# Half 1's second spectral stage as a class of its own, in buffers that the output stage shares

## The chip, the cores and the metric

The kernel runs on one core of a Trainium2 chip. The metric is the device time of one launch in microseconds (us). Before the change it was 2658.32 us, the median of three runs (2653.32 to 2668.18). The engines are called PE (matrix products), PEld (its weight loads), ACT (scalar engine), DVE (vector engine), POOL (GpSimd) and SP (the engine that issues most DMAs).

## The reference, cut to what matters

Layer 0 (a gated attention over 256 rows) makes x1, an image of 256 tokens of 256 x 128 pixels. Layer 1 takes those tokens through an attention in spectral space and two Fourier layers, and adds the result to x1. The change lies in the second Fourier layer (`mix_*[1]`) and the final sum:

```python
def spectral_conv(x, wr, wi, bias, out_hw):
    xf = jnp.fft.rfft2(x, norm='forward')
    top = jnp.einsum('bixy,ioxy->boxy', xf[:, :, :h, :m2], w[:, :, :h])
    bot = jnp.einsum('bixy,ioxy->boxy', xf[:, :, H - h:, :m2], w[:, :, h:])
    ...                                  # 32 x 16 modes, 4 channels in, 4 out
    return jnp.fft.irfft2(of, s=(Ho, Wo), norm='forward') + bias[:, None, None]

h1 = fno_layer(h0, mix_wr[0], ..., norm=True, act=True)
h2 = fno_layer(h1, mix_wr[1], ..., norm=True)
out = instance_norm(h2, mon_w, mon_b) + attn        # attn: normed sum of attention and tokens
```

A Fourier layer is a spectral product, normed, plus a 1x1 mixing of the four channels of a group ("skip"). Only 512 modes of each token are kept. The transforms are matrix products with small tables of sines and cosines; the norm of the spectral part is worked out from its modes.

## The kernel before, in words

The 256 tokens lie in two halves of 128, half 0 and half 1, one token to a partition. An image of a half is cut into 16 blocks of 2048 pixels (NB), each of two halves of 1024 (HB). In layer 1 a half goes through these steps, each a Python generator whose instructions are written out by hand in the order in which the engines are to take them (`manual_schedule`, L1890, for PE, ACT, DVE, POOL and SP): an engine takes its instructions, and SP its DMA issues, in the order of the program.

- `first_images` (L1582) makes the first layer's image block by block, transforms each block along the width into spectra and writes them to DRAM: psA (L1672) is copied by ACT to yA (L1674), and POOL issues the write to Yd (L1675), 16 image rows a block, 256 KB.
- `second_modes` (L1681) reads those spectra back (`load`, L1688, SP) into tiles YT of chunk c (four chunks of four frequencies) and half of the rows hc; `forward` (L1700) transforms along the height (L1706, into PSUM, copied by DVE to F, L1712); `mix_modes` (L1438) multiplies by the weights; `mixed` (L1475) copies the two accumulators to Z and squares them; `norm` (L1489) sums the energies; `synth_modes` (L615) transforms each chunk back along the height and writes it to Gd2 in DRAM (L664, SP and ACT issue two DMAs each); between the chunks stand the covariance (L1749), the blocks for the skip product (L1767), and at the end the per-token scale and shift (L1776 to L1786).
- `output` (L1788) makes the second layer's image of a block from the first layer's (skip, L1274) and the modes in Gd2 (image, L1259), scales it (L1795, ACT), adds w (L1801, DVE), and POOL issues the output DMA (L1802).

`mix_modes` works in products: DVE (every third one POOL) multiplies F by a weight, broadcast, into a tile (L1457), and PE adds it into an accumulator in PSUM by a product with the identity (L1470). For half 1 it takes two chunks at a time, two products to a tile; a group below is such a tile with its two accumulating products on PE.

w is lam * y + x1, where y is the attention's image (yd in DRAM) and x1 is read again. For half 1 class `Output1` makes it. `load(k)` (L1833) issues y and then x1 of 1024 pixels on SP (L1839, L1843); `add(k)` (L1846) makes w on DVE in one instruction (L1848). For k = 0 to 3 `ahead` (L1851) does this earlier, beside `second_modes`: ACT scales y (L1859) and POOL adds (L1863). In `run` (L1865) SP first issues the modes of four blocks (`modes`, four DMAs each, L1283), then `load` of k = 4 to 7, and then after each block b the modes of block b + 4, the adds of all loaded k up to 2b + 5, and the loads of 2b + 8 and 2b + 9.

A tile comes from a pool under a tag with a number of buffers. A new tile of a tag takes a buffer when the last reader of the tile that had it is done; the instruction that first writes it waits for that, also where that reader stands later in the program, on another engine. When a pool closes, its memory goes to pools opened later, and their first writers wait for its last users. Half 1's stage before uses pools of its own, opened after `with yctx` (L1899) has closed the pool xp, in which half 0's output and the loads lay: mp3 (YT and the transformed chunks, tag gt, two buffers), op1 (y under yo with two buffers, x1 under xo with five, two gs) and, for the output, op2 (three more yo, three more xo, two more gs).

The lines that set the order around the change:

```python
m1 = second_modes(1, wp, tiles(wp), Banks(psq, "q"), [(wp, "gt", 2)], [(wp, "gt", 2)] * 4)
next(m1)
o1.more = op
ahead = o1.ahead()
next(ahead)
next(ahead)
next(m1)
...
run(iter(lambda: next(m1), 1.2))
run(ahead)
run(m1)
```

Of the kernel before, what the change touches and what calls it, by code (L numbers as in the profile page):

```python
# [30 lines left out]
def rsqrt(nc, pool, out, var, eps, tag):  # L31

    shape = list(out.shape)
    ve = pool.tile(shape, FP, tag=tag + "_ve", name=tag + "_ve")
    nc.vector.tensor_scalar(ve, var, eps, None, ALU.add)
    r = pool.tile(shape, FP, tag=tag + "_r", name=tag + "_r")
    nc.scalar.activation(r, ve, AF.Sqrt)
    nc.vector.reciprocal(r, r)
    n = pool.tile(shape, FP, tag=tag + "_n", name=tag + "_n")
    nc.vector.tensor_mul(n, r, r)  # L40
    nc.vector.tensor_mul(n, n, ve)
    nc.vector.tensor_scalar(n, n, -0.5, 1.5, ALU.mult, ALU.add)
    nc.vector.tensor_mul(out, r, n)
# [544 lines left out]
def layer1(tc, I, C, ident, x1d, upool, U, Q2, groups, out):  # L588
# [9 lines left out]
    with ExitStack() as ctx:  # L598
# [983 lines left out]
        def first_images(a, wp, yp, psk, pst, first=None):  # L1582
# [44 lines left out]
            for b in range(17):  # L1627
# [37 lines left out]
                if b > 0:  # L1665
# [9 lines left out]
                    nc.gpsimd.dma_start(  # L1675
# [4 lines left out]

        def second_modes(a, wp, mk, psum, gts, yts):  # L1681

            h = halves[a]
            ym, yv, ra, lam, r2, rho, sig, _, kap, c0, hm, hv = (h.col[:, k : k + 1] for k in range(12))
# [29 lines left out]
            if a:  # L1714
                for hc in range(2):
                    for c in range(2):
                        load(c, (hc,))

                nc.scalar.activation(h.col[:, 12:13], yv, AF.Sqrt)
            else:  # L1720
                load(0)
# [3 lines left out]
            load(2 if a else 1)  # L1725
            yield 4.0
            forward(1)
            if not a:
                load(2)
# [14 lines left out]
            for c in range(4):  # L1744
                if c == 2:
                    ps = psum.tile(f"cvps_{a}")
                    for i in range(4):
                        for r in range(2):
# [7 lines left out]
                            queues=(nc.sync if a else nc.gpsimd, nc.scalar))  # L1756
# [4 lines left out]
                if c == 1:  # L1761
                    run(tail)

                    for i in range(4):
                        r = slice(32 * i, 32 * i + 32)
                        v = h.row[r, 0:P].rearrange("k (b d x) -> k b d x", b=2, d=2)
                        nc.vector.tensor_tensor(  # L1767
                            h.bl0[r].rearrange("k (b d x) -> k b d x", b=2, d=2),
                            v[:, :: (-1 if i & 2 else 1), :: (-1 if i & 1 else 1)],
                            bc(bc(blk[1][r, r], 1, 2), 1, 2), ALU.mult,  # L1770
                        )
            rs, krs, left = (h.col[:, k : k + 1] for k in (12, 14, 15))
# [3 lines left out]
            nc.vector.tensor_mul(krs, ps[:, 0:1], rs)  # L1776
            nc.vector.scalar_tensor_tensor(hv, krs, 4.0, hv, ALU.mult, ALU.add)
            nc.vector.tensor_add(hv, hv, left)
            rsqrt(nc, wp, kap, hv, EPS, "rq")
            nc.vector.tensor_mul(kap, kap, ch[:, 4:5])  # L1780
            nc.vector.tensor_mul(krs, kap, rs)
            nc.vector.tensor_mul(c0, hm, kap)
            nc.vector.tensor_sub(c0, ch[:, 5:6], c0)
            nc.vector.tensor_add(c0, c0, an[:, 1:2])
            nc.vector.tensor_mul(r2, ym, lam)
            nc.vector.tensor_sub(c0, c0, r2)  # L1786
# [40 lines left out]
        class Output1:  # L1827


            def __init__(self, wp):  # L1830
                self.wp, self.ld, self.w = wp, {}, {}

            def load(self, k):  # L1833
                px = slice(k * HB, (k + 1) * HB)
                old = k < 5 or k % 5 < 2
                y = (self.wp if old else self.more).tile(
                    [P, HB], FP, tag="yo", name=f"y4_{k}", bufs=2 if old else 3
                )
                nc.sync.dma_start(y, ydv[:, 1, px])  # L1839
                x = (self.wp if k % 8 < 5 else self.more).tile(  # L1840
                    [P, HB], FP, tag="xo", name=f"x4_{k}", bufs=5 if k % 8 < 5 else 3
                )
# [8 lines left out]
            def ahead(self):  # L1851

                for half in range(2):
                    for k in (2 * half, 2 * half + 1):
                        self.load(k)
                    yield
                    for k in (2 * half, 2 * half + 1):
                        y = self.ld[k][1]
                        nc.scalar.activation(y, y, AF.Identity, scale=halves[1].col[:, 3:4])  # L1859
                    yield  # L1860
                    for k in (2 * half, 2 * half + 1):
                        self.w[k], y = self.ld.pop(k)
                        nc.gpsimd.tensor_tensor(self.w[k], self.w[k], y, ALU.add)  # L1863

            def run(self, psk, more):  # L1865
                self.more = more
                gs = {}

                def modes(b):
                    gs[b] = (self.wp if b % 4 < 2 else self.more).tile(  # L1870
                        [P, 4, P], FP, tag="gs", name=f"gs3_1_{b}", bufs=2
                    )
                    load_modes(gs[b], halves[1].Gd2, b)

                for b in range(4):
                    modes(b)
                for k in range(4, 8):
                    self.load(k)
# [11 lines left out]
        with tc.manual_schedule(engines=COMPUTE | {ENG.SP}):  # L1890
# [8 lines left out]
            with yctx:  # L1899
                U1 = 24  # L1900
                with tc.tile_pool(name="mp0", bufs=1) as wp:
                    y1 = y_blocks(1, br, 0, U1, Sums(wp))
                    weave((2.4 * t for t in first_modes(0, wp, tiles(wp), bq, [(wp, "gt", 1)])), y1)
                    halves[0].sums = True
                    run(y1)
                with tc.tile_pool(name="hp0", bufs=2) as wp:
                    run(first_images(0, wp, xp, bq, br))
                with tc.tile_pool(name="mp1", bufs=1) as wp:
                    y1 = y_blocks(1, br, U1, 32)
                    next(y1)  # L1910
                    m0 = second_modes(
                        0, wp, tiles(wp), bq, [(xp, "xt", 3)], [(wp, "gt", 1)] * 3 + [(xp, "xt", 3)]
                    )
                    weave((2.4 * next(m0) for _ in range(3)), y1)
                    run(y1)
                    m1 = first_modes(
                        1, wp, Tiles(F=(xp, "yt", 2), f=(xp, "yt", 2), m=(xp, "gs", 3)), br, [(xp, "xt", 3)]
                    )
                    next(m1)
                    for k, _ in enumerate(iter(lambda: next(m0), None)):  # L1920
                        if k % 4 == 3:
                            next(m1)
                    for _ in m0:
                        next(m1, None)
                    o0 = output_0(bq)
                    next(o0)
                    y2 = wp.tile([P, NB], FP, tag="gt", name="y2_0", bufs=1)
                    nc.sync.dma_start(y2, ydv[:, 1, 0:NB])
                    run(m1)
                    g2 = wp.tile([P, 4, P], FP, tag="m", name="gs2_1_0", bufs=2)  # L1930
                    next(o0)
                    load_modes(g2, halves[1].Gd1, 0)
                    next(o0)
                with tc.tile_pool(name="hp1", bufs=2) as hp:
                    next(o0)
                    next(o0)
                    due, begun = 0.0, False
                    for done in first_images(1, hp, xp, bq, br, ([y2[:, 0:HB], y2[:, HB:]], g2)):
                        if not done:
                            due += 0.9  # L1940
                            begun = due > 0
                        if begun:
                            next(o0, None)
                        if done and begun:
                            due -= 1.0
                    run(o0)
            pz.release_now()
            with tc.tile_pool(name="op1", bufs=2, side="right") as op:
                o1 = Output1(op)
                with tc.tile_pool(name="mp3", bufs=1) as wp, tc.tile_pool(  # L1950
                    name="mpq3", bufs=8, space=PSUM
                ) as psq:
                    m1 = second_modes(1, wp, tiles(wp), Banks(psq, "q"), [(wp, "gt", 2)], [(wp, "gt", 2)] * 4)
                    next(m1)
                    o1.more = op
                    ahead = o1.ahead()
                    next(ahead)
                    next(ahead)
                    next(m1)
                    next(m1)  # L1960
                    next(ahead)
                    next(ahead)
                    run(iter(lambda: next(m1), 1.2))
                    run(ahead)
                    run(m1)
                with tc.tile_pool(name="opk1", bufs=8, space=PSUM) as psk, tc.tile_pool(
                    name="op2", bufs=1
# [166 lines left out]
```

## Time and profile before

| what | us |
|---|---|
| median of three runs (lowest, highest) | 2658.32 (2653.32, 2668.18) |
| the profiled execution | 2673.89 |
| its span, from the first to the last instruction | 2672.1 |
| last yA copy (L1674) ends | 2464.1 |
| first mixing product (L1457) begins | 2478.3 |
| last accumulating product (L1470) ends | 2504.0 |
| last instruction of the shift (L1786) ends | 2525.2 |
| first gs load for the output issued (L1283) | 2527.3 |
| first image product of the output (L1259) | 2529.6 |
| last output DMA issued (L1802) | 2665.6 |

The page's first line has the span; its part 1 gives the busy time of each engine, and part 2 cuts the span in 40 slices of 66.8 us. Layer 0 fills the first half, to about 1360 us; there PE, DVE and POOL are busy nearly all the time. Layer 1's spectral stages follow. The change touches what runs from about 2440 us to the end. In a timeline a line gives the start, the length, the engine, the line, what it writes and reads, the count of merged instructions, and in brackets the idle time before it with what ended it. PE's records are two for each product here. SPq, ACTq and POOLq are the engines' DMA issues; the time of a DMA itself is its landing, which the chain of work shows as "DMA out<-in".

### The profile page before, as it was taken

To read this page: it belongs to the slowest core of one execution; us is meant where nothing else is said; L and a number is where in the kernel's file an instruction comes from. 1 tells how busy PE (TensorE), PEld (TensorE's weight loads), DVE (VectorE), ACT (ScalarE), POOL (GpSimd) and SP (SyncE) were. 2 spreads that over 40 slices of the span, in tenths; PEclk is the share of its full clock that TensorE was granted. 3 is DMA by queue.
4 is the path that set the end of the run, shared out by engine and by line. 5 is a ranking of instruction groups with operands and counts; after the bars stand their busy time and mean duration, and the time that the engine had idled before them with its cause. 6 is when DMAs were issued, how large, how long until landed. Compare 5 with 4: busy or idle time off the path is not lost. (4 is left out here: it accounts for less than half of the span.)

```text
span 2672.1 us, 88760 instructions
## 1 busy us (share of the span) xinstructions
PE 2426.5 (91%) x37572; PEld 1549.0 (58%) x37572; DVE 2027.5 (76%) x2886; ACT 1421.3 (53%) x2718; POOL 1488.8 (56%) x1042
## 2 busy tenths in 40 slices
PE   6699999999999999999997999998979978898754
PEld 6555655555656555565554567786755456444533
DVE  6799999999999999999996457566546654465455
ACT  0278888888888888888884122001016401555232
POOL 1199999999999999999994012002136411111211
PEclk8899999999999999999998989999989988899855
DMA  9755666556566666565652011888877764997598
GB/s 348 222 91 100 107 105 107 101 104 105 105 105 109 107 107 108 102 106 103 109 101 63 4 58 47 274 272 289 297 264 265 239 223 149 332 359 260 192 386 344
DMA packets 1017925, 459.02 MB, mean 172 GB/s; under 512 B 831094, under 2 KB 947273, under 8 KB 1011128
## 3 DMA queue, kind: packets, MB, share of 16 engines
q1 hardware_dynamic: 977720, 363.13, 54.1%
q0 software_dynamic: 22912, 81.80, 7.9%
q10 hardware_dynamic: 16896, 8.39, 1.1%
q8 instruction: 298, 4.88, 0.8%
q14 instruction: 99, 0.81, 0.1%
HBM read 317.89 MB, written 135.27 MB: 170 GB/s over the span
## 5 line engine op out<-in xcount | busy, mean ns | idle before, releaser
L359 POOL TENSOR_TENSOR e<-e,b1T 128x1024 f32<-128x1024 f32 x256 | 607.1, 2372 | 143.8 <-DMA xk<-in_x_dram 76.2
L364 POOL TENSOR_TENSOR es<-e 128x512 f32<-128x512 f32 x512 | 648.4, 1289 | 0.0
L386 DVE RECIPROCAL av<-av 128x256 f32<-128x256 f32 x256 | 452.1, 1766 | 9.1
L342 ACT ACTIVATE sc<-sc,b2T 128x512 f32<-128x512 f32 x512 | 338.7, 662 | 122.9 <-PE sc L333 110.8
L342 ACT ACTIVATE e<-sc,b2T 128x512 f32<-128x512 f32 x512 | 324.7, 694 | 0.0
L354 DVE TENSOR_TENSOR e<-sc,b1T 128x1024 f32<-128x1024 f32 x256 | 310.9, 1215 | 9.7 <-ACT sc L342 9.3
L333 PE MATMUL sc<-qkT 32*128 32x256 f32 x4096 | 293.9, 400 | 3.4 <-DVE e L354 3.4
L1392 PE MATMUL yps<-xt,mpT 128*128 128x256 f32 x1024 | 252.8, 398 | 29.2 <-DVE yt L1404 12.6
L374 PE MATMUL av<-e,v 128*32 128x256 f32 x4096 | 269.1, 379 | 1.8 <-DVE gate L387 1.7
L333 PEld LDWEIGHTS sc<-qkT 32*128 32x128 f32 x4096 | 185.5, 184 | 115.2 <-issue 53.0
L1392 PEld LDWEIGHTS yps<-xt,mpT 128*128 128x128 f32 x1024 | 195.7, 197 | 75.4 <-DVE yt L1404 18.7
L374 PEld LDWEIGHTS av<-e,v 128*32 128x32 f32 x4096 | 130.0, 109 | 126.1 <-issue 38.3
L1408 POOL DMA_DIRECT2D yd<-yt x32 | 17.5, 546 | 320.2 <-DVE yt L1404 317.5
L308 ACT ACTIVATE qkT<-qk,qb 128x512 f32<-128x512 f32 x256 | 174.4, 681 | 7.5 <-PE qk L285 7.5
L285 PEld LDWEIGHTS u<-adft,x 128*32 128x32 f32 x4096 | 120.6, 111 | 82.7 <-issue 78.6
L285 PE MATMUL qk<-turned,wn_wq 128*32 128x256 f32 x2048 | 164.5, 393 | 1.8 <-DVE turned L293 1.8
L410 ACT ACTIVATE turned<-turned 128x256 f32<-128x256 f32 x256 | 104.4, 408 | 113.7 <-DVE x1b L396 111.4
L379 PE MATMUL av<-es,ones 128*32 128x256 f32 x2048 | 161.1, 379 | 1.6 <-POOL es L364 1.6
L285 PE MATMUL qk<-turned,wT_wk 128*32 128x256 f32 x2048 | 158.4, 381 | 0.0
L293 DVE STREAM_TRANSPOSE turned<-xk 128x1024 f32<-128x1024 f32 x128 | 157.9, 1234 | 0.1
L1795 ACT ACTIVATE blocks<-h2ps,col 128x512 f32<-128x512 f32 x128 | 88.9, 777 | 128.3 <-PE h2ps L1259 128.3
L285 PE MATMUL u<-adft,x 128*32 128x129 f32 x4096 | 139.5, 276 | 6.2 <-DMA x<-x1d 6.2
(532 smaller groups left out, 4177.7 us busy)
## 6 DMA issues: line engine op xcount, KB each, us to landing
xt<-x1d SPq DMA_DIRECT2D x128, 512.0 KB, 7.8
xb<-in_x_dram SPq DMA_DIRECT2D x32, 1024.0 KB, 7.8
xk<-in_x_dram SPq DMA_DIRECT2D x512, 64.0 KB, 3.1
xk<-in_L_conv_kv_x_dram SPq DMA_DIRECT2D x512, 64.0 KB, 2.5
x1d<-x1b SPq DMA_DIRECT2D x512, 64.0 KB, 2.2
x<-x1d SPq DMA_DIRECT2D x128, 256.0 KB, 3.2
y<-yd SPq DMA_DIRECT2D x62, 512.0 KB, 6.3
gs<-Gd SPq DMA_DIRECT2D x384, 64.0 KB, 5.3
```

Source lines behind the costliest of these rows:

```text
L285: nc.tensor.matmul(out[hd], w[:, hd], src, start=start, stop=stop)
L293: nc.vector.transpose(turned[:, a : b + 1 : b - a].rearrange("p k (b c) -> p k b c", c=32), t)
L308: nc.scalar.activation(r["qkT"], ps, AF.Identity, bias=self.qb)
L333: nc.tensor.matmul(sc[h // 2][:, h % 2, c * 256 : (c + 1) * 256], qkT[p, 256 + c * P : 256 + (c + 1) * P], qkT[p, 0:256], start=True, stop ...
L342: nc.scalar.activation(r["e"][1][:, :, c, :] if hp else z, z, AF.Exp, bias=b2T[:, c, s : s + 1])
L354: nc.vector.tensor_tensor(r["e"][0].rearrange("p h c q -> p (h c q)"), r.pop("sc").rearrange("p h x -> p (h x)"), b1T[:, 0:2].rearrange("p ...
L359: nc.gpsimd.tensor_tensor(e1, e1, b1T[:, 2:4].rearrange("p h c q -> p (h c q)"), ALU.mult)
L364: nc.gpsimd.tensor_tensor(es, e[:, :, 0, :], e[:, :, 1, :], ALU.add)
L374: nc.tensor.matmul(ps[hd, 0:256], p["v"][:, 2 * (s % 2) + c, hd], r["e"][h // 2][:, h % 2, c, :], start=(c == 0), stop=(c == 1),)
L379: nc.tensor.matmul(ps[32 * h : 32 * h + 32, 256:512], self.ones, r["es"][h // 2][:, h % 2, :], start=True, stop=True,)
L386: nc.vector.reciprocal(rd, rd)
L1392: nc.tensor.matmul(rows_of(ps[j]), mpT[:, sc, tt], by_turn(xt[:, sc])[:, j], start=(sc == 0), stop=False,)
```

## The change

Half 1 no longer uses `second_modes`. A class `LastModes` does the same work in one method, `run`, and is called between `first_images` of half 1 and the output. In parts:

- **Spectra.** `LastModes.load` issues the loads of Yd in eight DMAs: the rows 0 to 127 as two tiles of 1 MB in the tag xt, the other rows as three tiles (two in yt, one in xt), each first for rows 128 to 239 and then for the last 16. The pool xp stays open to the end (`yctx` is no longer closed), so those are the buffers of half 0's output and of half 1's first images. The last block's write of Yd is issued by ACT, not POOL.
- **Forward transform.** All products with rows 0 to 127 come first, for all four chunks, then those with the other rows; two chunks share a PSUM bank.
- **Mixing.** DVE reads F from PSUM; ACT copies F to SBUF for POOL (groups 2 and 5 of 8) and the covariance. Three buffers for products instead of two. Chunks 0 and 1 are mixed first (`group(0, n)`); then ACT copies them out and squares them, and the inverse transform of chunk 1 stands between the third and the fourth group of chunks 2 and 3. All products of one k in `group` go into two accumulators as before.
- **Inverse transforms.** In the order 1, 0, 2, 3; all four DMAs of a chunk are issued by SP; PSUM copies are shared as `engines` says. The energies come ahead of chunk 3, and everything that follows from them (row, covariance, blocks, shift) after chunk 3.
- **y and x1 for the output.** `o1.load(0)` and `load(1)` come after the first half of the mixing, `load(2)` and `load(3)` between chunk 2 and chunk 3. Their adds are four instructions of DVE at the start of `Output1.run`, after the four `modes`; ACT's scaling and POOL's adds are gone. x1 and w lie in tiles of a whole block (three xt buffers, one gt), y in two yt buffers for k = 0 to 3, and in two ya and two yt buffers from there on. gs has three buffers in xp and two in the pool op.
- **rsqrt** (L31, used in all stages) has one DVE instruction less.

The diff, cut:

```diff
@@ rsqrt
-    nc.vector.tensor_mul(n, r, r)
-    nc.vector.tensor_mul(n, n, ve)
+    nc.vector.scalar_tensor_tensor(n, r, r, ve, ALU.mult, ALU.mult)
@@ first_images
-                    nc.gpsimd.dma_start(
+                    (nc.scalar if a and b == 16 else nc.gpsimd).dma_start(
@@ new
+        class LastModes:
+            def load(self):
+                tile = lambda tag, bufs, n, name: xp.tile([P, 2, n], FP, tag=tag, name=name, bufs=bufs)
+                rows = halves[1].Yd.rearrange("h (r f) t -> h r (f t)", r=2)
+                self.low = [tile("xt", 3, 1024, f"YT0_{k}") for k in range(2)]
+                for k in range(2):
+                    nc.sync.dma_start(self.low[k], rows[0:P, :, 1024 * k : 1024 * k + 1024])
+                self.high = [tile("yt", 2, 512, f"YT1_{k}") for k in range(2)] + [tile("xt", 3, 1024, "YT1_2")]
+                at = (slice(0, 512), slice(512, 1024), slice(1024, 2048))
+                for lo, hi in ((0, 112), (112, P)):
+                    for t, c in zip(self.high, at):
+                        nc.sync.dma_start(t[lo:hi], rows[P + lo : P + hi, :, c])
...
+            def synth(self, c, banks, gt, engines):
...
+                for f in range(4):
+                    (nc.vector.tensor_copy if engines[f] else nc.scalar.copy)(gt[:, f, :], banks[f])
...
+                        nc.sync.dma_start(
+                            halves[1].Gd2[r0 : r0 + 4, 2 * jp : 2 * jp + 2].rearrange("f j g t -> (j g) f t"),
+                            gt[:, :, k * P : (k + 1) * P],
+                        )
+            def run(self, psq, o1):
...
+                for hc in range(2):
+                    for c in range(4):
...
+                                    nc.tensor.matmul(
+                                        fw[c // 2][32 * f : 32 * f + 32, c % 2, r, :],
...
+                for k in range(2):
+                    nc.scalar.copy(
+                        F[:, 2 * k : 2 * k + 2].rearrange("p c r t -> p (c r t)"),
...
+                def group(k, n):
+                    made = xp.tile([P, 2, 2, G, 4], FP, tag="gs", name=f"z1m_{k}_{n}", bufs=3)
+                    pool = n % 3 == 2
+                    for q in range(2):
...
+                        src = F[:, 2 * k : 2 * k + 2] if pool else fw[k]
...
+                        (nc.gpsimd if pool else nc.vector).tensor_tensor(
+                            made[:, q], bc(f, 3, 4), bc(w, 2, G), ALU.mult
+                        )
+                    for q in range(2):
+                        nc.tensor.matmul(
+                            acc[n % 2][:, 2 * k : 2 * k + 2, :], ident, made[:, q].rearrange("p c g o -> p (c g o)"),
...
+                for n in range(8):
+                    group(0, n)
+                for r in range(2):
+                    nc.scalar.copy(Z[:, 1, r, :], acc[r][:, 1])
+                nc.scalar.activation(Z[:, 0, 0, :], acc[0][:, 0], AF.Identity, scale=z0)
+                nc.scalar.activation(Z[:, 0, 1, :], acc[1][:, 0], AF.Identity, scale=wsyn[:, 0:1])
+                squares(0)
+                gt0 = gts(0)
+                o1.load(0)
+                o1.load(1)
+                for n in range(3):
+                    group(1, n)
+                self.synth(1, four(1), gts(1), (0, 0, 0, 0))
+                nc.scalar.activation(F[:, 0], F[:, 0], AF.Identity, scale=hw0)
+                for n in range(3, 8):
+                    group(1, n)
+                nc.scalar.copy(Z[:, 2:4, 0, :], acc[0][:, 2:4])
+                nc.vector.tensor_copy(Z[:, 2:4, 1, :], acc[1][:, 2:4])
+                self.synth(0, four(0), gt0, (0, 1, 0, 1))
+                squares(2)
+                self.synth(2, four(2), gts(2), (0, 1, 0, 1))
+                o1.load(2)
+                o1.load(3)
+                en = bank("f", 2, "z1ens")
...
+                self.synth(3, ..., gts(3), (0, 1, 0, 1))
+                rsqrt(nc, op, rs, en[:, 0:1], EPS, "rq")
...
+                shift(op, h, en[:, 3 * P : 3 * P + 1])
@@ Output1.load
+                if k % 2 == 0:
+                    self.blocks[b] = (
+                        self.op.tile([P, NB], FP, tag="gt", name=f"w1_{b}", bufs=1) if b % 4 == 3
+                        else xp.tile([P, NB], FP, tag="xt", name=f"w1_{b}", bufs=3)
+                    )
+                y = (
+                    self.op.tile([P, HB], FP, tag="ya", name=f"y4_{k}", bufs=2) if k >= 4 and k % 4 < 2
+                    else xp.tile([P, HB], FP, tag="yt", name=f"y4_{k}", bufs=2)
+                )
@@ Output1.run
                 for b in range(4):
                     modes(b)
+                for k in range(4):
+                    self.add(k)
                 for k in range(4, 8):
                     self.load(k)
```

## The prediction, made before the changed kernel was run

> **What bounds the kernel now.** I read the stage table first, then the chain of work that ended last, then what SP's queue waited for. From the last spectrum of half 1 to the end there are four stages. In the rows below the first column is the stretch, then come its length, the busy time of PE, PEld, DVE, ACT and POOL with counts, the granted clock, the DMA share and GB/s.
>
> ```profile
> 2463.50:2486.70 23.20, 10.41 (x197) 7.94 (x197) 6.46 (x9) 4.37 (x5) 6.74 (x5) 0.71 0.84 298
> 2486.70:2504.10 17.40, 16.63 (x128) 12.27 (x124) 8.08 (x21) 3.38 (x4) 8.04 (x9) 1.00 0.18 70
> 2504.10:2525.20 21.10, 14.99 (x324) 13.43 (x324) 13.90 (x43) 5.30 (x11) 3.41 (x2) 0.90 0.64 176
> ...
> 2544.20:2672.10 127.90, 63.97 (x736) 39.70 (x736) 68.64 (x57) 33.42 (x48) 16.02 (x30) 0.54 0.96 367
> ```
>
> The last 128 us move 367 GB/s with the DMA engines 0.96 busy: the output of half 1 is bound by bytes. Nothing in its loop saves time unless it saves bytes, and the change saves none. So the change can only move **the moment at which this full traffic begins**, and the bytes that are over by then. Ahead of it lie 62 us of latency, and the chain says which:
>
> ```profile
> 2464.40 3.52 DMA Yd<-yA
> 2468.07 4.24 DMA YT<-Yd
> ...
> 2475.77 8.16 DMA YT<-Yd
> ...
> 2513.96 5.09 DMA Gd<-g21gt
> ...
> 2522.06 4.90 DMA Gd<-g21gt
> ```
>
> Spectra written, spectra read back, read back again for chunks 2 and 3 (queued behind four y and x1 loads), then the mixing, then the inverse transforms' writes of Gd2. The first image begins at 2529.6, when its modes land. SP's queue shows one more thing, and it decides my forecast:
>
> ```profile
> 2541.40 1.28 DVE L1848 SCALAR_TENSOR_TENSOR x<-y,col,x 128x1024 f32<-128x1024 f32 x1 [3.83 <-DMA x<-x1d]
> 2542.71 0.32 SPq L1839 DMA_DIRECT2D y<-yd  x1
> ```
>
> ```profile
> SPq L1839 <- DVE x L1848: 3.8, 1, 3.8
> ```
>
> y4_6 shares its buffer with y4_4, whose one reader, add(4), comes later in the program. SP keeps program order, so it stood 3.8 us until DVE had done add(4), and everything behind it stood too.
>
> **What the Trainium skill says.** "TensorE: Matmul & The Clock Gate", part 1: an idle window of some 3.4 us halves TensorE's clock, and the same time of work restores it. The trace agrees: the clock was 0.50 from 2468 to 2476, and 48 of L1706's records took 2.79 us there against 64 in 1.96 us at full clock. "PSUM — Partial Sum Buffer", PSUM bank collisions: two engines must not touch one bank together, two readers included, and software keeps them apart. The trace agrees: ACT's square (L1486) of an accumulator waited 0.96 us for DVE's copy (L1481) of the same bank. "DMA: Bandwidth & Descriptors", issuing engines are not separate DMA queues: a transfer moved to ACT runs on the same 16 engines. Here too: ACT's and SP's writes of Gd2 together ran at 287 GB/s. "VectorE: DVE Perf Modes", why PSUM operands drop a tier: fp32 from PSUM runs at the plain rate, and so does any tensor_tensor; so a product from PSUM should cost what one from SBUF costs. Before has no such product, but L1712 copied 256 elements out of PSUM in 0.42 us and L1457 multiplied 256 in SBUF in 0.42.
>
> **The change part by part.** All moments are on the clock of the profiled execution.
>
> *Early spectra.* SP's first YT load waited 14.3 us for output writes (out_dram<-w), since its tiles lay on memory of closed pools. Now the lower 128 rows go into xt buffers from about 2444 on, rows 128 to 239 when block 14's Yd lands (issued 2459.6, so near 2463), and only 16 rows wait for the last Yd. Its issue on ACT follows yA's copy (ends 2464.1) directly; landing after 3.0 to 3.9 us (POOL's took 3.52): 2467.7. The 16-row loads cost what a 64 KB gs load costs, 2.3 us, plus their issue: 2470.3. The 1.83 MB of rows 128 to 239 need 4.6 us at 400 GB/s (the loads of 2478 to 2488 ran at 390 to 409) and are in by 2469. The forward matmuls of rows 0 to 127 are over at 2468; the others are 128 records: 3.9 us at full clock, 7.4 at half. PE is idle only 2.2 us, so I take 4.5 and a little more for the late chunks: **2475.5**. This removes the 8.16 us re-read.
>
> *Mixing.* Before, 15 groups took 2486.7 to 2504.0, less 2.0 us of L1706: 1.02 us each, with PE busy 16.6 of 17.4 us. PE sets this pace, not the products (two DVE instructions are 0.7 to 0.8 us). So products from PSUM gain nothing by themselves; they save F's copy ahead of the first product (0.42 us), and no scaling on POOL lies beside them, which once stretched a product to 1.99 us. Eight groups: 8.2. Then ACT reads both accumulators (four 128x128 pieces of about 0.25 us, squares of about 0.4); being in the banks that the next set writes, they hold PE about 1.5 us (0 if only addresses counted, 2.2 at most). Three groups 3.1, chunk 1's transform 2.1 (L641), five groups 5.1, POOL's pairs 0.5 (0.53 was the usual wait for one): **2496.0**, against 2504.0.
>
> *Inverse transforms.* Chunk 0: 2.1 to 2498.1; copies 1.3, during which chunk 2 lacks its four banks; chunk 2 ends 2501.5; energy sums (L1495) 1.9; chunk 3 2.1, 2505.5; copies 1.3, 2506.9. DVE has these ahead of rsqrt: 1.55 (1.73 less one instruction of 0.19), four small ones 0.9: 2509.4. The row product and the covariance, now in one bank after those readers: 0.6 and 2.6 (L1508, L1749, clock 0.51 before and again here): 2512.8. Turned blocks 1.2, cv 0.3, its sum 0.6, and hand-overs: 2515.1. The shift 3.4 (4.7 before, less 1.3 that ACT stood behind copies): **2518.5**, against 2525.2. So far 6.7 us are won.
>
> *The new hold.* o1.load(2) comes ahead of chunk 3's writes in SP's order. y4_2 takes the yt buffer of y4_0, and y4_0's reader is add(0), which DVE now does after the shift (L1859 on ACT and L1863 on POOL, which freed it early, are gone). So SP stands from chunk 2's writes (some 2505) until 2518.5 + 1.3 = 2519.8 (L1848 is 1.28), and for load(3) until 2521.1. **Queued behind it**: chunk 3's four Gd2 writes, then all 16 gs loads, then load(4). The 2.1 MB of loads 2 and 3 go first: from 2521.2, 1.3 us after issue (a gs load lands in 1.9 at the least), at 400 GB/s 5.3 us; then 1.05 MB of Gd2 at 287 GB/s, 3.7, and half a us of receipt: 2530.6 for the first gs load, **3.3 us later** than before (2527.3). Bounds: a shift ending 6 us earlier (no hold by ACT, warm PE) makes it -3; a cold forward (+3) and more hand-overs make it +8. In exchange load(6) no longer waits for add(4): before, that cost no more than 0.7 us of DMA time, since loads and two outputs (3.1 MB) filled those 8 us. The 16 gs issues (7.9 us) and the rest are the same in both.
>
> *The rest.* One instruction less in rsqrt, 0.19 us, some ten times earlier in the program: 0 to 1.9, hidden behind PE or DMA work in most; I take 0. The squares, z0 and F's scaling on ACT replace DVE instructions of 0.2 to 2.4 us that were not last; without that cover they'd cost 1 us. POOL loses four adds, 9.5 us beside other work.
>
> **Sum.** +3.3 - 0.7 = +2.6 us on a profiled execution of 2673.9 us (span 2672.1): 2676.5. The median of the runs is 15.6 lower, 2658.3; the same 2.6 there gives **2661**. With the bounds, 2655 to 2667.
>
> **Rivals.** *Hold without effect, faster.* If y4_2 finds its buffer free, or chunk 3's writes get ahead of it, they land at 2506.9 + 4.9 = 2511.8, gs at 2514, and the stage waits for the shift alone, 2518.5; load(4) is issued near 2520 instead of 2535.4. Full traffic begins 14 to 15 us sooner: 2644. For it: the path to the shift is shorter. Against: the 3.8 us above, by the same rule. Chance 0.20, with an earlier shift than I think beside it.
>
> *The output loop gets slower.* x1 now comes in tiles of two halves, so an x load needs both outputs of a block landed, not one; the second is issued 1.13 us after the first. At block 11 it was issued at 2637.4 and lands 7.2 to 8.7 us later, 2644.6 to 2646.1; the load that needs it was issued at 2647.9. The slack is 1.8 us or more, so I expect nothing; if landing grows beyond 10.5 us, twelve blocks lose about 1.1 each, 13 us: 2674. y has four buffers for five, and no more than four were in use. Chance 0.16.
>
> *Nothing moves but the work* is the likeliest case itself: 0.64.
>
> **From these to the numbers.** A measurement of this kernel tells about 0.5%, 13.3 us, from no change. The likeliest case lies within it whole; the rivals fall just outside. Leaving the outer half of each rival out gives 2643 to 2672, which holds a little over 8 in 10.
>
> **What would show it.** SP idle from about 2505 to 2520 with add(0) as releaser, and Gd2's last write landing after 2529. Spectra landed by 2471. Mixing at 1.02 us a group. PE held about 1.5 us between the sets. DMA share 0.96 and 9.0 us a block in the loop (outputs of blocks 10 and 11 were issued at 2627.22 and 2636.25). The forecast is wrong if y4_2 is issued before the shift, if the loop's block takes over 9.5 us, or if the shift ends before 2512.

## The result, and the profile after

The changed kernel took 2670.8 us, the median of 13 runs, against 2661.6 us for the kernel before in the same comparison (13 runs): a ratio of 1.0025, with a 95% interval of 1.0011 to 1.0039. The two medians are 9.2 us apart; the ratio stands for about 7 us. So the kernel with the rewritten stage is no faster but a little slower, within the 0.5% that the prediction called no change.

The profiled executions must be lined up before they are compared. In the twelve profiles of this document the 2.45 ms ahead of the last spectra differ by up to 18 us, and by 11 us between kernels whose code is the same up to there. So all moments below are counted from A, the end of the last copy of yA (L1674 in before, L1673 in after): 2464.12 in before, 2457.88 in after.

| us after A | before | forecast | after |
|---|---|---|---|
| last Yd write landed | 3.8 | 3.6 | 9.1 |
| spectra read back whole | 19.8 | 6.2 | 12.0 |
| forward transform of the spectra over | 28.6 | 11.4 | 17.9 |
| last accumulation of the mixing over | 39.9 | 31.9 | 35.5 |
| shift over | 61.1 | 54.4 | 58.4 |
| first output load (gs) issued | 63.2 | 66.5 | 70.9 |
| load(4) issued | 71.2 | - | 79.0 |
| end of the span | 208.0 | - | 216.7 |

(In before the last 64 records of the forward transform, chunk 3's, lie between the groups of the mixing.) The table shows where the time goes. The mixing ends 4.4 us sooner than before and the shift 2.7 us sooner; then the first gs comes 7.7 us later, and the lead has become a loss. From gs to the end both kernels take nearly the same: 144.8 and 145.8 us.

The stages of after, in the columns of the prediction's first fence (stretch, length, busy time and count of PE, PEld, DVE, ACT and POOL, granted clock, DMA share, GB/s):

```profile
2457.90:2475.80 17.90, 9.63 (x257) 8.76 (x257) 3.47 (x7) 2.07 (x3) 1.19 (x2) 0.71 0.65 186
2475.80:2493.40 17.60, 16.45 (x132) 13.78 (x132) 7.56 (x20) 5.01 (x13) 3.57 (x6) 1.00 0.25 90
2493.40:2516.30 22.90, 16.27 (x261) 13.52 (x260) 9.50 (x37) 4.19 (x10) 0.00 (x0) 0.68 0.41 121
2516.30:2530.60 14.30, 0.01 (x1) 0.02 (x1) 5.02 (x5) 0.00 (x0) 0.00 (x0) 0.50 0.74 229
...
2544.00:2674.60 130.60, 65.07 (x736) 40.33 (x736) 69.68 (x58) 34.65 (x50) 15.97 (x30) 0.56 0.96 364
```

The fourth row is new: 14.3 us in which PE has one instruction, ACT and POOL have none and DVE is busy a third of the time. The last row is the output loop, 364 GB/s at a share of 0.96, as before.

The chain of work that ended last (start, length, what) shows the two places that matter:

```profile
2457.90 9.12 DMA Yd<-yA
...
2467.04 2.79 DMA YT<-Yd
2469.87 5.92 PE f1ps L1856 x128
2475.80 7.12 PE z1acc L1884 x32
...
2483.73 0.28 ACT z1sq L1898
2484.05 2.86 PE z1acc L1884 x12
...
2521.09 7.54 DMA Gd<-g21gt
...
2528.76 1.79 DMA gs<-Gd
```

Two DMAs stand out. The first line is the 256 KB write of the last spectrum, 9.12 us from issue to landing; 3.52 in before. The 7.54 us of Gd2 are the last of chunk 3's writes, and they start only at 2521. Why so late is on SP's queue. Its waits between 2430 and the end (us in total, times, longest), and its timeline:

```profile
SPq L2012 <- DVE w L2019: 14.5, 1, 14.5
```

```profile
2491.01 12.03 SPq L1833 DMA_DIRECT2D Gd<-g21gt  x12
2517.59 0.33 SPq L2012 DMA_DIRECT2D y<-yd  x1
...
2519.74 3.93 SPq L1833 DMA_DIRECT2D Gd<-g21gt  x4
2528.76 8.07 SPq L1282 DMA_DIRECT2D gs<-Gd  x16
2536.92 0.37 SPq L2012 DMA_DIRECT2D y<-yd  x1
```

SP issued chunk 2's writes by 2503.0, met load(2), and stood 14.5 us, until add(0) (L2019) had read the buffer that y4_2 takes. DVE had copied chunk 3's modes into SBUF by 2504.9. Their writes were issued from 2519.74 on, after the loads of blocks 2 and 3, and all 16 gs loads came behind them.

### The profile page after: what moved, and what is told of

The parts are those of the page before. It is cut to its first block, busy times and chain, and to the rows that moved or that the text cites. A ratio compares the mean times of both kernels' runs of the same rounds, so it can differ in the third digit from the quotient of the medians.

```text
span 2674.6 us, 88727 instructions
## 1 busy us (share of the span) xinstructions
PE 2418.3 (90%) x37572; PEld 1549.9 (58%) x37572; DVE 2022.2 (76%) x2873; ACT 1414.8 (53%) x2725; POOL 1473.0 (55%) x1035
## 5 line engine op out<-in xcount | busy, mean ns | idle before, releaser
L1391 PEld LDWEIGHTS yps<-xt,mpT 128*128 128x128 f32 x1024 | 194.1, 195 | 75.1 <-DVE yt L1403 22.5
L1969 POOL DMA_DIRECT2D out_dram<-w x64 | 34.2, 534 | 202.4 <-DVE w L1968 202.2
```

The costliest lines, as they stand in the source:

```text
L1391: nc.tensor.matmul(rows_of(ps[j]), mpT[:, sc, tt], by_turn(xt[:, sc])[:, j], start=(sc == 0), stop=False,)
```

## The experiments

Two theories stood against each other. **The hold decides**: half 1's stage is shorter, but SP's order gives it all back, and the late write of the spectra adds to it. **The stage decides**: products from PSUM, the interleaved transform or the new order of loads cost time themselves, and the hold only fills what would be idle anyway. Each edit is to the changed kernel. Ratios are to the kernel before, timed beside each edited kernel, with 95% intervals; they rest on 4 runs (rows 0 to 127 late) to 22 of the edited kernel, the moments on one profiled execution each. Moments are from A, as above. (The chain of "loads 2, 3 last, split" does not reach back to the write; its landing is taken from the reads that SP issued on it, at 2451.77.)

| kernel | last Yd landed | gs issued | load(4) issued | end | ratio |
|---|---|---|---|---|---|
| before | 3.8 | 63.2 | 71.2 | 208.0 | 1 |
| after | 9.1 | 70.9 | 79.0 | 216.7 | 1.0025 (1.0011 to 1.0039) |
| adds 0, 1 early | 10.1 | 58.1 | 66.4 | 203.8 | 0.9953 (0.9936 to 0.9969) |
| loads 2, 3 last | 9.8 | 52.1 | 62.1 | 200.3 | 0.9969 (0.9958 to 0.9981) |
| last Yd by POOL | 9.5 | 71.6 | 79.8 | 216.4 | 1.0027 (1.0016 to 1.0039) |
| rows split 96/32 | 4.0 | 65.5 | 74.1 | 209.2 | 1.0001 (0.9988 to 1.0013) |
| both, loads between | 5.3 | 48.3 | 59.1 | 193.5 | 0.9953 (0.9933 to 0.9972) |
| products from SBUF | 10.4 | 71.9 | 80.2 | 216.3 | 1.0022 (1.0007 to 1.0038) |
| rows 0 to 127 late | 9.6 | 80.0 | 88.2 | 223.3 | 1.0076 (1.0056 to 1.0095) |
| no interleaving | 10.2 | 72.1 | 80.2 | 216.0 | 1.0026 (1.0014 to 1.0038) |
| loads 2, 3 last, split | 4.4 | 46.7 | 57.2 | 199.3 | 0.9955 (0.9934 to 0.9976) |
| adds early, split | 5.2 | 55.0 | 63.2 | 200.3 | 0.9947 (0.9926 to 0.9968) |

**Adds early.** Undo the hold without touching the order of SP's queue: add(0) and add(1), which need only their loads, go ahead of load(2) in the program.

```diff
                 self.synth(2, four(2), gts(2), (0, 1, 0, 1))
+                o1.add(0)
+                o1.add(1)
                 o1.load(2)
                 o1.load(3)
@@ Output1.run
-                for k in range(4):
+                for k in range(2, 4):
                     self.add(k)
```

> Edit: add(0) and add(1) stand ahead of load(2) in the program, where DVE idles between chunk 2's and chunk 3's copies; nothing else. A is the end of the last yA copy. Hold theory: y4_2 is issued about A+45 instead of A+59.7, chunk 3's Gd2 writes land by A+54, the first gs load is issued at A+55 (changed kernel A+70.9, kernel before A+63.2), load(4) at A+63 to 64 instead of A+79. Time 14 to 16 us below the changed kernel, so a ratio to the kernel before near 0.997. Late-spectra theory (the loss is the spectra that landed 5.9 us late): the shift ends as before at A+58 and the time is within 3 us of the changed kernel, ratio 1.002. Output-loop theory: also as the changed kernel.

```profile
2481.09 12.27 SPq L1833 DMA_DIRECT2D Gd<-g21gt  x12
2493.47 0.65 SPq L2014 DMA_DIRECT2D y<-yd  x1
...
2496.03 4.25 SPq L1833 DMA_DIRECT2D Gd<-g21gt  x4
2505.12 8.14 SPq L1282 DMA_DIRECT2D gs<-Gd  x16
```

On SP's timeline y4_2 now follows the last of chunk 2's writes by 0.1 us (2481.09 + 12.27 = 2493.36; issue at 2493.47). The hold is gone, gs comes 12.8 us sooner after A than in after, and the span ends 12.9 us sooner. (gs was expected at A+55 and came at A+58.1: the loads of blocks 2 and 3 still stand ahead of chunk 3's writes, the last of which took 7.90 us to land.) In the timed runs the two kernels differ by 0.72%, 19 us. So the hold costs the changed kernel 12.9 us by the moments and somewhat more by the runs: without it the change makes the kernel faster by 0.3 to 0.6%.

**Loads last.** The same hold, removed by order: loads 2 and 3 go behind the gs loads and behind the first two adds.

```diff
-                o1.load(2)
-                o1.load(3)
@@ Output1.run
-                for k in range(4):
-                    self.add(k)
+                self.add(0)
+                self.add(1)
+                self.load(2)
+                self.load(3)
+                self.add(2)
+                self.add(3)
```

> Edit: load(2) and load(3) moved behind the 16 gs loads and behind add(0) and add(1); the hold by the yt buffers stays but nothing that the first image needs is queued behind it, and the early loading of k = 2 and 3 is given up. Hold theory: gs from A+52 to 60, y4_2 at A+60, then six loads without a pause; full traffic begins 19 us sooner than in the changed kernel with 2.1 MB (5.3 us) more to move: 12 to 14 us below the changed kernel, ratio to before near 0.998. If early loading itself were what counts, this would be no faster than the changed kernel.

gs comes at A+52.1, 18.8 us sooner than in after, since now the 2.1 MB of loads don't stand ahead of chunk 3's writes either: the last of these writes landed in 3.28 us, where it took 7.54 in after. The end is 16.4 us sooner by moments, and 0.56% (15 us) by the timed runs.

**Last Yd by POOL.** Is the slow landing of the last spectrum due to its issue on ACT? The write goes back to POOL's queue.

> Edit: the last block's write of Yd is issued by POOL again; nothing else. Contention theory (the write lands 9.1 us after issue because 1.8 MB of spectra loads run beside it): landing within 1 us of the changed kernel's, the spectra at A+12, time unchanged within 2 us. Queue theory (ACT's queue is the slow one): landing at A+4 to 5 as POOL's before, spectra 4 to 5 us sooner, time about 4 us below the changed kernel.

The write, in the chain of this kernel, which it enters at its issue on POOL:

```profile
2450.53 9.20 DMA Yd<-yA
```

9.20 us against 9.12: the issuing queue makes no difference, and the time does not move (1.0027).

**Rows split 96/32.** Then what runs beside it? In after, SP issued the loads of rows 128 to 239 at 2456.28, 1.6 us ahead of the write. With the split at 96, rows 128 to 223 need only spectra that were written one block earlier.

```diff
-                for lo, hi in ((0, 112), (112, P)):
+                for lo, hi in ((0, 96), (96, P)):
```

> Edit: the second half of the rows is loaded as rows 128 to 223 and then the last 32, instead of 112 and 16. The first part need not wait for the last block but one, so it is over when the last Yd is written. Contention theory: the write of Yd lands at A+3 to 4, the last 0.5 MB at A+6.5 to 7.5 instead of A+12, all that follows 4 to 5 us sooner, time 4 to 5 us below the changed kernel. If the landing of Yd has another cause: no change in its 9 us, and the time as the changed kernel.

The chain of this kernel, and then, in the columns of the stage table, its 4 us after A:

```profile
2446.87 4.00 DMA Yd<-yA
2450.93 2.94 DMA YT<-Yd
```

```profile
2446.90:2450.90 4.00, 3.70 (x128) 3.46 (x128) 0.00 (x0) 1.49 (x2) 0.00 (x0) 1.00 0.35 98
```

The loads were issued 7.3 us before A and were all but over when the write began (0.11 MB of that queue are left in these 4 us): the DMA engines are 0.35 busy, and the write lands in 4.00 us. In after, in contrast, the write has the loads of the upper rows beside it. DMA by queue (packets, MB, share of the 16 engines; q1 is SP's loads, q10 the write), first from 2457.9 to 2462.5, then from 2462.5 to 2467.1:

```profile
q1 hardware_dynamic: 519, 1.11, 91.5%
q10 hardware_dynamic: 3, 0.00, 0.2%
...
q1 hardware_dynamic: 189, 0.70, 53.5%
q10 hardware_dynamic: 525, 0.26, 21.6%
```

The Trainium skill says in "DMA: Bandwidth & Descriptors", section on queues, rings and completion order, that a DMA engine with work on several queue rows goes round them packet by packet. By that the write's packets should go through among those of the loads from the start. This trace does not show it: in the first 4.6 us after its issue the write moved 3 of its 528 packets while the loads moved 519, and the other 525 went in the second half, as the loads ran out. With the split, 507 went in the first 2 us. The write issued on POOL behaves the same: none of its packets moved in its first 4 us. So the late landing is mostly a wait behind the loads that were issued 1.6 us sooner; what keeps the write back is not shown.

With the split gs comes 5.4 us sooner, and the ratio is 1.0001, which agrees with the moments (209.2 against 208.0): with this one line the changed kernel equals the one before, hold and all.

**Both.** Adds early, rows split, and loads 2 and 3 between chunk 3's writes and gs.

```diff
-                for lo, hi in ((0, 112), (112, P)):
+                for lo, hi in ((0, 96), (96, P)):
@@
-                o1.load(2)
-                o1.load(3)
+                o1.add(0)
+                o1.add(1)
@@ after chunk 3's synth
+                o1.load(2)
+                o1.load(3)
```

> Edit: three together: rows split at 224 (the last 32 late), add(0) and add(1) ahead of chunk 3, load(2) and load(3) behind chunk 3's writes but ahead of the gs loads. If hold and contention are two separate losses, both come back: spectra at A+7, shift at A+54, gs issued by A+52, load(4) at about A+60, end near A+197 to 200 (changed kernel A+216.7, kernel before A+208.0). Ratio to the kernel before 0.991 to 0.993. If the hold was the only loss and the split is hidden once it is gone: as e1, 0.995.

By moments this is the shortest of all: gs at A+48.3, end at A+193.5. In the timed runs it only equals the early adds alone (0.9953), where 0.991 to 0.993 had been expected. Its chain, from the adds to the first modes' landing:

```profile
2486.10 2.39 DVE w L2021 x2
2488.49 1.50 issue
2490.00 1.29 DVE g21gt L1828 x2
...
2496.45 6.47 DMA gs<-Gd
2502.97 2.36 PE h2ps L1258 x26
```

Two limits are close now. The early adds (2.39 us) and a gap of 1.5 us stand ahead of DVE's copy of chunk 3 (L1828), whose writes follow. And the first modes land at 2502.92, while DVE has the shift only at 2502.5 and begins add(2) at 2502.62: an earlier gs alone would find the shift as late as itself.

**Products from SBUF.** Does reading the spectra from PSUM cost the mixing anything? DVE multiplies from F instead.

```diff
-                        src = F[:, 2 * k : 2 * k + 2] if pool else fw[k]
+                        src = F[:, 2 * k : 2 * k + 2]
```

> Edit: DVE's mixing products take F from SBUF (ACT's copy) instead of PSUM; nothing else. PE-pace theory: the products are ready ahead of PE either way, first product at the same moment since DVE waits for ACT's read of that bank in any case; last accumulation within 1 us of the changed kernel's A+35.5, time unchanged. PSUM theory (reading PSUM is what made 8 groups take 7.2 us instead of 8.2): products slow down beside POOL's, the mixing takes 2 us or more longer.

The 12 products of the largest group, first in after and then in this kernel (out<-in, shapes, count; then busy us, mean ns):

```profile
L1880 DVE TENSOR_TENSOR z1m<-f1ps,mixwr 128x256 f32<-128x256 f32 x12 | 5.0, 419 | 8.7 <-ACT F L1863 4.2 <-PE z1acc L1884 4.1 <-issue 0.2
```

```profile
L1880 DVE TENSOR_TENSOR z1m<-F,mixwr 128x256 f32<-128x256 f32 x12 | 5.3, 440 | 8.4 <-PE z1acc L1884 4.1 <-ACT F L1863 4.0
```

From PSUM a product takes 419 ns, from SBUF 440; in the other two groups of six the means rise from 423 and 414 to 491 and 488. The shortest are the same (411 and 413). What differs is the start of the mixing, where DVE and POOL work at the same time: there single products of DVE took up to 0.84 us and POOL's first two 0.85 and 0.79, against 0.61 in after. PE did not wait for it: the first set of eight groups takes 7.12 us of PE's chain in both kernels, and the time is the same. The source of the products is worth nothing in time here, as the prediction had it.

**Rows 0 to 127 late.** Undo the early loads: the two loads of the lower rows go behind those of the upper ones.

```diff
-                for k in range(2):
-                    nc.sync.dma_start(self.low[k], rows[0:P, :, 1024 * k : 1024 * k + 1024])
...
                         nc.sync.dma_start(t[lo:hi], rows[P + lo : P + hi, :, c])
+                for k in range(2):
+                    nc.sync.dma_start(self.low[k], rows[0:P, :, 1024 * k : 1024 * k + 1024])
```

> Edit: the two loads of rows 0 to 127 are issued after those of the other rows, so behind the last write of Yd; this undoes the early loading alone. If the early loads are worth what was forecast, the spectra are complete at A+17 instead of A+12, the forward transform of all rows comes after that, cold at first, its end 7 to 9 us later than A+17.9, and the time 7 to 9 us above the changed kernel. If the queue hides it: within 2 us.

The chain now has all the spectra's forward matmuls in one piece behind the loads:

```profile
2461.50 6.17 DMA YT<-Yd
2467.80 9.27 PE f1ps L1856 x256
```

The forward transform ends at A+27.2 instead of A+17.9, and gs comes 9.1 us later. The end comes 6.6 us later by moments; the timed runs, only four, show 0.51%, 14 us, and the two intervals leave some 7 to 20 us. So the early loads are a gain of about the 7 to 9 us that were expected; it is not they that made the change a loss.

**No interleaving.** All eight groups of the second set, then chunk 1's transform.

```diff
-                for n in range(3):
+                for n in range(8):
                     group(1, n)
                 self.synth(1, four(1), gts(1), (0, 0, 0, 0))
-                for n in range(3, 8):
-                    group(1, n)
```

> Edit: the inverse transform of chunk 1 stands behind all eight groups of the second set instead of between the third and the fourth. PE does the same work; chunk 0's transform then waits for ACT's four copies of chunk 1 (2 us). Shift about 2 us later than A+58.4, time 1 to 3 us above the changed kernel. If the interleaving only filled time in which PE worked anyway: no change.

The mixing ends at A+34.0 instead of A+35.5, but one more transform is then left to do: the shift ends at A+59.5 instead of A+58.4, and gs comes at A+72.1 against 70.9. The time is the same (1.0026). Whatever the interleaving gains ends in the hold or is below what can be told.

**Loads last, split** and **adds early, split.** Two runs to see whether the two savings add in the other combinations too.

> The changed kernel with two edits: loads 2 and 3 behind chunk 3's writes and the first output loads, and behind add(0) and add(1); rows split 96/32. In the kernels so far the span ends 143.3 to 145.8 us after the first issue of an output load (gs), 148.2 with this order. If the two savings add (the hold is off SP's queue, so the first gs follows the last Gd2 write; the split brings the spectra 5.2 us sooner): first gs at A+46.7 (52.1 - 5.4), end at A+195, 13 us before the kernel before's A+208.0: ratio 0.995. If without the hold another thing decides when chunk 3 is written (an eviction, the rate of the transfers): gs not below A+51, end about A+199, ratio 0.9965, as without the split.

> The changed kernel with two edits: add(0) and add(1) ahead of load(2); rows split 96/32. If the time follows the first gs after A, and the two add: first gs at A+52.7 (58.1 - 5.4), end at A+198 (145.5 later), 10 us before the kernel before: ratio 0.996, slower than the run with loads 2 and 3 after chunk 3's writes by some 4 us. If the ratio of 0.9953 that the early adds alone gave was their true worth, and more than their moments show: 0.9953 - 0.0024 for the split = 0.993.

With the loads last, gs came at A+46.7 to the tenth, but the end at A+199.3 and not 195. The stretches of its stage table show a part of why, in the columns as above:

```profile
2496.00:2502.00 6.00, 4.91 (x82) 2.97 (x98) 4.65 (x20) 0.42 (x2) 0.00 (x0) 0.50 0.42 120
2502.00:2510.00 8.00, 8.00 (x202) 3.84 (x177) 2.00 (x2) 7.56 (x12) 0.00 (x0) 0.88 0.90 288
```

SP spends 8.4 us on issuing the 16 gs loads, which move only 1 MB: from 2496 to 2502 the DMA engines ran at 120 GB/s, while 2.1 MB of y and x1 stood behind them in SP's order. In the kernel of both, where those loads go first, the stretch from 2496 to 2502 ran at 381 GB/s. But then that kernel was the slower one, and from 2480 to 2520 it moved only some 0.6 MB more, worth 1.6 us at the 372 GB/s of its loop (an estimate), of the 5.8 us by which the two ends differ. With the loads last SP also stood 5.0 us again, in front of y loads whose buffer an add had yet to read. The rest is open, and the timed runs do not tell the two kernels apart. With the early adds and the split, gs came at A+55.0 (52.7 expected), since the write of Yd took 5.1 us and the forward transform of the upper rows 6.6, at a granted clock of 0.50 for the first 4.6 of them. The two ratios, 0.9955 and 0.9947, cannot be told from 0.9953: **the four kernels with the hold removed that reach 0.995 are equal within their intervals**, and all beat both the kernel before and the changed one. That the split is worth anything once the hold is gone is seen in the moments alone.

## Why the prediction was right, and where it was off

*What bounds the kernel: right.* The last stage moves the same bytes at the same rate whatever comes before it. In ten of the twelve kernels the end follows the first gs by 143.3 to 145.8 us, while gs itself moves over 31.7 us. The two exceptions, 148.2 and 152.6, are those that put loads 2 and 3 behind gs.

*The new hold: right, and shown.* The prediction had 12.1 us from the shift to the first gs; it was 70.9 - 58.4 = 12.5. SP stood with add(0) as releaser until 2517.6, chunk 3's writes landed at 2528.6, and two independent ways to remove the hold each bring gs forward by 12.8 us or more. The change was no loss by its own stage: that was 2.7 us shorter at the shift, and with the hold removed it is a gain. The rival "hold without effect" described the kernel that the change could have been; its 2644 would be a ratio of 0.9946, and the kernels without the hold measured 0.9947 to 0.9969.

*Early spectra: the term that was mis-sized.* The step reads "landing after 3.0 to 3.9 us (POOL's took 3.52)" and, two sentences on, that 1.83 MB of loads move at the same time. Each was priced as if alone. The write took 9.1 us, because it stood behind those loads, so the spectra were whole at A+12.0 instead of A+6.2. PE then stood idle 8.2 us instead of 2.2, its granted clock was 0.50 from 2466 to 2474, and the 128 forward records took 5.92 us instead of 4.5; the bound of 7.4 was not needed. Together +6.5. The prediction quoted the Trainium skill on the 16 engines that all queues share ("DMA: Bandwidth & Descriptors", issuing engines are not separate DMA queues), but only for the change of the issuing queue; the same sentence bears on the loads beside the write.

*Mixing: too dear, by 1 us in the first set, and before was misread.* Eight groups took 7.2 us, not 8.2: 0.90 a group. The step says that PE set the pace before, and weighs only DVE's two products of 0.7 to 0.8 us. But the chain of before goes through POOL's products as well, and its waits from 2486 to 2504 have PE's weight loads waiting for them (us in total, times, longest):

```profile
2493.83 0.87 POOL z1m L1457
...
2494.74 1.14 PE z1acc L1470 x4
...
2496.02 0.87 POOL z1m L1457
```

```profile
PEld z1acc L1470 <- POOL z1m L1457: 2.7, 5, 0.6
```

In after the chain of the mixing has PE's accumulations alone (7.12 us in one piece above). Three things differ there: POOL makes both products of two groups in eight instead of every third product, each takes 0.61 us instead of 0.86, and there is a third buffer, so that they can be made further ahead. Which of these frees PE was not tried; it isn't only that DVE reads PSUM (7.12 us with F from SBUF too). PE was held by ACT's reading 1.15 us against 1.5. The step "POOL's pairs 0.5" has no wait of its own in PE's list of waits between A and the shift: 0. Sum: -2.9 against the forecast from the forward to the last accumulation (17.6 us instead of 20.5).

*Inverse transforms to the shift: right.* 22.9 us, 22.5 forecast.

*The output loop: right that little changes, wrong on load(6).* The wait for add(4) is gone, and 0.7 us were booked as won; gs to the end became 1.0 us longer. The block-wise tile, the place of the second rival, did bite once:

```profile
SPq L2014 <- DMA out_dram<-w: 5.0, 1, 5.0
```

That is one x load, early in the loop, that waits for an output of an earlier block, and not twelve of them.

*The sum.* In moments the forecast was +2.6 us and the two profiles show +8.7: +4.4 by the first gs (6.5 - 2.9 + 0.4, and 0.4 in the hold), 0.7 for load(6), 1.0 in the loop. The timed runs show +0.25%, 6.7 us (2.9 to 10.4). So the total came out near the forecast partly by luck: +6.5 on the spectra and -2.9 on the mixing are errors of opposite sign. The median, 2670.8, is inside the 2643 to 2672 of the prediction by 1.2 us only, and outside the 2655 to 2667 of its likeliest case; the kernel before was itself 3.3 us slower here than in the three runs from which the forecast starts, and the ratio on those gives 2665. The rsqrt term (0 to 1.9 us) can't be seen below the 11 us by which executions of the same code differ ahead of A.

*What stays open.* The early adds alone end 4.2 us sooner than before by moments, which is 0.16%, and measured 0.31 to 0.64% faster; with the split 7.7 us, 0.29%, against 0.32 to 0.74%. The profiled execution is one, and part of the gain of these two kernels is not in the stretch after A of that one.

## What to carry to other kernels

A load placed early in an in-order queue is early only if its buffer is free by then: look up the last reader of the tile it takes over, and where that reader stands on its own engine; whatever is queued behind the load waits too. Price a small transfer on the critical path with what was issued shortly before it, not from a row where it ran alone; loads that can be issued one step earlier should be over by then. When a stage is rewritten and the time stands still, compare the moments of hand-over from a common point: the lead and the place where it is given back are then two rows of a table.

## What was not expected of the hardware

A 256 KB write took 3.5 us with little beside it (before, share 0.37), and 4.0 to 5.3 in the four kernels with the rows split 96/32, but 9.1 to 10.4 us when 1.8 MB of loads had been issued on another queue 1.6 to 1.9 us earlier, from ACT's queue as from POOL's. It did not share the engines with them from the start: 3 of its 528 packets moved in the first half of its 9.1 us. The DMA engines showed a share of 0.86 then, at 231 GB/s, where the output loop reaches 364 at 0.96: their busy share alone doesn't tell how many bytes they move.

```profile
2458.00:2467.00 9.00, 3.70 (x128) 3.43 (x128) 0.00 (x0) 1.49 (x2) 0.00 (x0) 0.85 0.86 231
```
